# A two-layer kernel (a state-space layer, then an outlook-attention layer): where the first two attention tiles are made

## The chip, the core and the metric

The kernel runs on one core of a Trainium2 chip. The core has five engines that run their own instruction streams, each in the order in which it was given: PE (TensorE, the matrix multiplier; the profile shows its weight loads apart, as PEld), DVE (VectorE), ACT (ScalarE), POOL (GpSimd) and SP (SyncE), which here issues nearly all DMA transfers. They meet through semaphores only. Data lie in SBUF (on the chip, 128 partitions) and in HBM; matmuls write to PSUM, an accumulation memory of eight banks for each partition.

The metric is the time of one execution in microseconds on the device. Lower is better.

## What is computed

Input `x` is (4, 384, 64, 64) in float32. Two residual layers follow each other, each on a group norm of its input: a state-space layer over the 4096 pixels of an image, in sequence, and outlook attention on 3x3 windows with stride 2:

```python
    x = x + _L0_conv_ref(_gn(x), L0_conv_ln_w, L0_conv_ln_b, L0_conv_in_proj_w, L0_conv_conv_w, L0_conv_conv_b, L0_conv_x_proj_w, L0_conv_dt_w, L0_conv_dt_b, L0_conv_A_log, L0_conv_D, L0_conv_out_proj_w)
    x = x + _L1_conv_ref(_gn(x), L1_conv_attn_w, L1_conv_attn_b, L1_conv_conv_w, L1_conv_proj_w, L1_conv_proj_b)
```

Layer 0 normalises, projects 384 channels to twice 768, convolves along the sequence, makes step sizes `dt` and the vectors B and C, runs for each of 768 channels a scan with 16 states over 4096 steps (`h = dA * h + dBx`, `y = sum(h * C)`), gates it and projects back to 384.

Layer 1, cut to its core (12 heads of 32 channels, windows of 3x3 = 9 places, 32x32 windows in an image; `a` are the weights, `v` the values made from the patches with one matrix for each place, and the last addition is the fold, in which overlapping windows add up):

```python
        pooled = x.reshape(B, C, h, S, w, S).mean(axis=(3, 5))
        a = jnp.einsum('bchw,ac->bhwa', pooled, attn_w) + attn_b
        a = a.reshape(B, L, HEADS, K * K, K * K).transpose(0, 2, 1, 3, 4) * scale
        a = jax.nn.softmax(a, axis=-1)
...
        v = jnp.einsum('blkc,koc->blko', v, Wg)
        v = v.reshape(B, L, K * K, HEADS, hd).transpose(0, 3, 1, 2, 4)
        o = jnp.einsum('bnlpq,bnlqd->bnlpd', a, v)
...
                out = out.at[:, :, ki:ki + S * (h - 1) + 1:S, kj:kj + S * (w - 1) + 1:S].add(o[:, :, ki, kj])
...
        y = jnp.einsum('bchw,oc->bhwo', out, proj_w) + proj_b
```

The group norm at the head of layer 1 needs mean and variance of all that layer 0 gives for an image; so the last image's coefficients exist only when layer 0 is over, while those of the first three are there long before.

## The kernel before

**Layer 0** (`mamba_layer`) cuts each image's sequence into 17 chunks of 241 steps, 68 chunks in all. A chunk has 12 units of scan work (a unit: 2 groups of 32 channels with 16 states). The main loop (from L776) takes one step `s` for each unit. In a step DVE runs two scans (`s_scan`), ACT makes the decays of the next unit in two PSUM tiles `da0` and `da1` (`s_decay`, tiles from L559), POOL makes inputs and outputs (`s_inputs`, `s_outputs`), and every second step PE sums the states into `y` (`s_sum`) and DVE gates it (`s_gate`). SP fetches the inputs of two units four steps ahead (`s_fetch`: `dxr`, `dtr`). The front of a chunk (norm, projections, convolution) is laid into the steps of the chunks before by a table `plan`; what ends a chunk (`ends`: `e_project` with the output projection `ps_out` into `xr`, then `e_store` with the statistics and the store to `x1` in HBM) follows in the steps after it. `group_norm_coeffs` (L50) makes an image's coefficients `sc` and `bi` from these statistics: aggregation on DVE (`mv`), `pm` and `pv` on PE, a power on POOL, `bi` on ACT.

Engines work strictly in the order of the program text (class `InOrder`): an instruction that waits holds up all behind it on its engine, and a DMA that waits on SP all DMAs behind it.

**Layer 1** (`outlook_layer`) works on 32 tiles of 8 image rows (4 rows of windows, 128 windows). For a tile: load of 9 rows of `x1` as `xr` (864 KB; 768 KB for the first tile of an image), normed pixels `xp` (6 activations on ACT), pooled sums `t2` (3 additions on DVE), weights (`psa`: 6 matmuls, 12 in the records; softmax on DVE and ACT in tile `at`; store to an HBM tile `ad`), values (`psv`: 9 places of 3 matmuls, 54 records in all; copies on ACT; stores to `vd`). Then for each of the four rows of windows `r`: fetch of weights and values from HBM as `ain` and `vin`, a block-diagonal form `bd` of the weights (on ACT for even `r`, on POOL for odd `r`), products `ps` on PE, `fold` on DVE; last the projection `pso` and the output. The loop at L1085 takes three tiles at a time: it attends tile `i`, makes weights and values of tile `i+1`, and at `r == 2` the pixels of tile `i+2`. In an iteration PE has, in order: `psa` and the first three values of the next tile, `pso` of the tile before, products of `r = 0`, two values, products of `r = 1`, two values, and so on.

**Between them** stands the generator `outlook_before` (L1116). The main loop sends it on once in each step from `front_end` (step 803) to the last (step 839), through `behind` (L1206). By then the SBUF room of the fronts has been given back; the generator uses this room. It gets two PSUM buffers from the loop's pool `pmm`, which the projections use as well. Before, it loads tile 0 and the value matrices `wv`, makes pixels, values and pooled sums of tile 0, then those of tile 1, and then loads `wa` (1458 KB), `ab`, `wpr`, `pb`, `own` into the room that it used so far. In steps 814 and 815 the last units are scanned; the steps behind hold the last sums, gates, projections and the norm.

`outlook_layer` then starts with a scale of `wa` by 0.25 on DVE (L924) and, for tiles 0 and 1 (list `ready`), a second load of their rows for the residual and the weights (L1082), one tile after the other. The first iteration of the loop after that (`i = -1`) only fetches tile 0's weights and makes its first `bd`; the second (`i = 0`) attends tile 0, with no values to be made.

Of the kernel before, what the change touches and what calls it, by code (L numbers as in the profile page):

```python
# [7 lines left out]
F32 = mybir.dt.float32  # L8
# [4 lines left out]
P = 128  # L13
# [66 lines left out]
def mamba_layer(ctx, tc, x, w, x1, sc1, bi1, consts, behind):  # L80
# [475 lines left out]

    das = [pda.tile([P, NG * (1 + TM)], F32, tag=f"da{i}", name=f"da{i}") for i in range(2)]  # L559
    for da in das:  # L560
        ve.memset(da.rearrange("p (g s) -> p g s", g=NG)[:, :, 0:1], 0.0)
    bp = pbb.tile([P, 2, TM], F32, tag="bp", name="bp")
    ND = NG // 2
    units = {}
# [211 lines left out]
    for s in range(-4, NU * (len(chunks) + 2)):  # L776
        k, m = divmod(s, NU)
        if m % 2 == 0 and unit(s + 4) is not None:
            s_fetch(s + 4)
        parts(s, EARLY)  # L780
        if m % 4 == 3 or s >= NU * len(chunks):
            norm_part(False)

        if (u := unit(s + 1)) is not None:
            s_inputs2(u)
        if (u := unit(s - 3)) is not None and not u.first:
            s_gate(u)
        parts(s, READY)

        b, ci = chunks[k][:2] if 0 <= k < len(chunks) else (B, 0)  # L790
        if b + 1 < B:
            n, e = divmod(NU * ci + m - 3, NU // 2)
            if e == 0 and 0 < n <= NCB * NX:
                x_stat(b + 1, n - 1, pending.pop())
            if e == 1 and 0 <= n < NCB * NX:
                pending.append(x_load(b + 1, n))
            if e == 2 and n == NCB * NX:
                x_coeffs(b + 1)
        for i in range(2):
# [12 lines left out]
        norm_part(True)  # L812
        parts(s, POOL)
        if (u := unit(s + 2)) is not None:
            s_inputs(u)
        if (u := unit(s - 2)) is not None and not u.first:
            s_sum(unit(s - 3), u)
        parts(s, MID)
        parts(s, LATE)
        if s == front_end:  # L820
            fronts.close()
        if s >= front_end:
            behind(lambda: pmm.tile([P, 2, TM], F32, tag="mm", name="psv").rearrange("p a b -> p (a b)"))


NR = 4
# [3 lines left out]
class OutlookTile:  # L830
# [52 lines left out]
    def pool(self, ve, t2, t3):  # L883
# [13 lines left out]
def outlook_layer(ctx, tc, x1, w, out, sc1, bi1, weights, ready):  # L897
# [10 lines left out]
    NW = W // 2  # L908
    NT = H // (2 * NR)
    HO = HEADS * KK  # L910
    NA = HO * KK
    NH = NA // 2
    NGW = 3
    VQ = 3
    scale = float(HD) ** -0.5
    pe, ve, ae, gp, sp = (
        InOrder(tc, e) for e in (nc.tensor, nc.vector, nc.scalar, nc.gpsimd, nc.sync)
    )
# [1 line left out]
    wa, ab, wv, wpr, pb, own, vds, ads = (  # L920
        weights[name] for name in ("wa", "ab", "wv", "wpr", "pb", "own", "vds", "ads")
    )

    ve.tensor_scalar_mul(wa, wa, 0.25)  # L924
    io = ctx.enter_context(tc.tile_pool(name="io1", bufs=3))
    act = ctx.enter_context(tc.tile_pool(name="act1", bufs=2))
    pa = ctx.enter_context(tc.tile_pool(name="pa", bufs=1, space=bass.MemoryType.PSUM))
# [14 lines left out]
        c.pool(ve, t2, t3)  # L942

    def p_weights(c):

        psa = pa.tile([P, 2, 512], F32, tag="psa", name="psa")
        for h in range(2):
            for cb in range(NCB):
                pe.matmul(
                    psa[:, h, :NH],  # L950
                    c.t2[:, cb, :],
                    wa[:, cb, h * NH : (h + 1) * NH],
                    start=(cb == 0),
                    stop=(cb == NCB - 1),
                )
        at = act.tile([P, NA], F32, tag="at", name="at")
        ve.tensor_add(at.rearrange("p (h a) -> p h a", h=2), psa[:, :, :NH], ab.rearrange("p (h a) -> p h a", h=2))
        qs = at.rearrange("p (q a) -> p q a", q=KK)
        mx = act.tile([P, HO], F32, tag="mx", name="mx")
        ve.reduce_max(mx, at.rearrange("p (q a) -> p a q", q=KK), AX.X)  # L960
        ve.tensor_sub(qs, qs, mx.unsqueeze(1).to_broadcast([P, KK, HO]))
        ae.activation(at, at, AF.Exp, scale=scale)
        rs = act.tile([P, HO], F32, tag="rs", name="rs1")
        ve.reduce_sum(rs, at.rearrange("p (q a) -> p a q", q=KK), AX.X)
        ve.reciprocal(rs, rs)
        ve.tensor_mul(qs, qs, rs.unsqueeze(1).to_broadcast([P, KK, HO]))
        sp.dma_start(ads[c.i % 2][: P * KK, :].rearrange("(p q) a -> p (q a)", q=KK), at)

    def p_values(c, q):

# [108 lines left out]

        return (old, r) if r < NR else (mid, r - NR)  # L1080

    for c in ready:  # L1082
        p_load(c)
        p_weights(c)
    for i in range(-1, len(tiles) + 1):  # L1085
        new, mid, old = tile_at(i + 2), tile_at(i + 1), tile_at(i)
        for r in range(NR):
            if old and r == 0:
                p_fetch_values(old, 0)
            if old and r + 1 < NR:  # L1090
                p_fetch_values(old, r + 1)
            if mid and r == 0 and mid not in ready:
                p_weights(mid)
            c, k = ahead(old, mid, r + 2)
            if c:
                p_fetch_weights(c, k)
            c, k = ahead(old, mid, r + 1)
            qs = ((0, 1, 2), (3, 4), (5, 6), (7, 8))[r]
            for n, q in enumerate(qs):
                if c:  # L1100
                    p_blocks(c, k, n, len(qs))
                if mid and mid not in ready:
# [12 lines left out]

def outlook_before(ctx, tc, w, x1, H, W, sc1, bi1, dram, weights, ready):  # L1116


    nc = tc.nc
# [7 lines left out]
    t2s = [wp.tile([P, NCB, NR * NW], F32, tag=f"t2{i}", name=f"t2{i}") for i in range(2)]  # L1127
    with tc.tile_pool(name="before", bufs=1, side="right") as early:

        zero = early.tile([KK, C], F32, tag="zero", name="zero")  # L1130
# [4 lines left out]
        def load(i):  # L1135
            ready.append(OutlookTile(i, H, W))
            ready[i].load(sp, x1, early.tile([P, NCB, ROWS, W], F32, tag="xr", name="xr"))

        def pixels(i):
            return ready[i].pixels(gp, ae, early.tile([P, 3, NCB, ROWS, NW], F32, tag="xp", name="xp"), sc1, bi1)  # L1140

        def value(i, q):
            ps = psum()
            ready[i].values(pe, wv, q, ps[:, :C])
            v = early.tile([P, C], F32, tag="v", name="v", bufs=4)
            ae.copy(v, ps[:, :C])
            sp.dma_start(vds[i][: P * KK, :].rearrange("(p q) c -> p q c", q=KK)[:, q, :], v)

        load(0)
        made = pixels(0)  # L1150
        for q in range(KK):
            sp.dma_start(wv[:, :, q, :], w["wv"][:, :, q, :])
            if q % 2:
                psum = yield
                next(made, None)
        for i in range(2):
            if i == 1:
                for _ in pixels(1):
                    psum = yield
            for q in range(KK):  # L1160
                value(i, q)
                if q == 0 and i == 0:
# [6 lines left out]
            psum = yield  # L1169
    wp = ctx.enter_context(tc.tile_pool(name="wp1", bufs=1, side="right"))  # L1170
    na = HO * KK
    shapes = {
# [5 lines left out]
    }  # L1178
    for name, shape in shapes.items():
        weights[name] = wp.tile(shape, F32, tag=name, name=name)  # L1180
        sp.dma_start(weights[name], w[name])


@with_exitstack
def layers(ctx, tc, w, out):
# [17 lines left out]
    weights, ready = {}, []  # L1203
    later = outlook_before(ctx, tc, w, x1, H, W, sc1, bi1, dram, weights, ready)

    def behind(psum):  # L1206
        try:
            later.send(psum if started else None)
        except StopIteration:
            pass  # L1210
        started.append(True)
# [70 lines left out]
```

## Time and profile before

| | us |
|---|---|
| three runs | 6302.01, 6313.15, 6318.55 |
| their median | 6313.15 |
| the profiled execution, its own time | 6318.34 |
| its span in the profile | 6316.6 |

| engine | busy us in the whole span | share |
|---|---|---|
| PE | 5629.0 | 89% |
| DVE | 5369.9 | 85% |
| POOL | 5311.1 | 84% |
| ACT | 4986.2 | 79% |

| event of the stage between the layers | us from the start |
|---|---|
| first transfer for layer 1 (tile 0's rows) issued | 4968.96 |
| first value of tile 0 on PE | 4993.27 |
| last value of tile 1 ends on PE | 5064.30 |
| load of `wa` issued | 5067.64 |
| coefficients of the last image (`bi`) done | 5080.49 |
| second load of tile 0's rows issued | 5080.52 |
| first attention product `ps` of tile 0 | 5115.99 |
| first attention product of tile 1 | 5153.89 |
| first attention product of tile 2 | 5191.75 |
| end of the span | 6316.6 |

How to read the lines further down: `L45` is the line of the helper through which all engines' instructions go, so tiles tell the operations apart, by the names above. `out<-in` is followed by the shapes and `xN`, the number of instructions in the group. A float32 matmul leaves two records. In brackets stands how long the engine had been idle before, and what released it. PEclk is the clock that the core granted to PE, as a share of full speed.

### The profile page before, as it was taken

The numbers are of one execution on the slowest core, as the hardware profiler recorded it, in microseconds if no ns is written. First come the engines' busy times: TensorE is split into PE (matmuls) and PEld (weight loads), VectorE is DVE, ScalarE is ACT, GpSimd is POOL, SyncE is SP. The second block draws the span as 40 slices with busy tenths as digits, with TensorE's granted clock in tenths as the row PEclk, the third lists the DMA queues.
The fourth block names the chain that finished last, engine by engine and source line by source line (L and its number), as shares of the span: only waits on it lengthen the run. The fifth ranks groups of instructions, "written<-read, shape, count | busy, mean of one in ns | idle before, by whom it ended". The sixth has DMA issues, their size and how long they took to land.

```text
span 6316.6 us, 113361 instructions
## 1 busy us (share of the span) xinstructions
PE 5629.0 (89%) x40488; PEld 3968.2 (63%) x40488; DVE 5369.9 (85%) x4784; ACT 4986.2 (79%) x11842; POOL 5311.1 (84%) x2047
## 2 busy tenths in 40 slices
PE   6888888898888888888888898988988779999999
PEld 5666666666666666666666666666666445555555
DVE  4999999999999999999999999999999844544444
ACT  3888888888898888888888888989888734444453
POOL 3999999999999999999999999999999924333333
PEclk9899989999998999999999989999999789999999
DMA  4555555455555555555555455554555544445544
GB/s 129 130 133 146 149 130 137 128 138 141 146 131 143 135 136 137 135 131 145 136 146 148 122 135 131 140 139 125 137 129 137 154 144 164 166 166 171 169 165 143
DMA packets 640987, 895.10 MB, mean 142 GB/s; under 512 B 130265, under 2 KB 535179, under 8 KB 640164
## 3 DMA queue, kind: packets, MB, share of 16 engines
q1 hardware_dynamic: 640420, 887.84, 51.5%
q8 instruction: 319, 5.23, 0.4%
q14 instruction: 248, 2.03, 0.1%
HBM read 661.78 MB, written 225.70 MB: 141 GB/s over the span
## 4 chain that ended last, share of the span: by engine, by line
PE 23%; ACT 17%; DVE 11%; issue 3%; DMA 1%; POOL 1%; SPq 1%; ACTq 0%; DVEq 0%; POOLq 0%
ACT da L45 10%; DVE h L45 8%; PE psv L45 6%; PE pso L45 4%; PE ps L45 4%; PE psa L45 3%; PE y L45 2%; PE ps_in L45 1%; ACT xc L45 1%; DVE at L45 1%; PE ps_xd L45 1%; DVE mx L45 1%; ACT L45 1%; POOL h L45 1%; ACT dt L45 1%
## 5 line engine op out<-in xcount | busy, mean ns | idle before, releaser
L45 DVE TENSOR_TENSOR_SCAN h<-da,h 128x968 f32<-128x968 f32 x1632 | 3449.4, 2154 | 80.9 <-issue 52.7
L45 ACT ACTIVATE da<-dtr,aneg 128x241 f32<-128x241 f32 x6528 | 3036.5, 465 | 291.9 <-DVE h L45 128.4
L45 POOL TENSOR_TENSOR h<-h,bc 128x1928 f32<-128x1928 f32 x816 | 3228.2, 3956 | 11.0 <-DVE h L45 8.8
L45 POOL TENSOR_TENSOR h<-dxr,bc 128x964 f32<-128x964 f32 x816 | 1625.6, 1992 | 116.8 <-PE y L45 101.3
L45 PE MATMUL ps_in<-u,win 128*128 128x241 f32 x4896 | 1079.6, 374 | 82.0 <-DVE dtx L45 75.1
L45 PEld LDWEIGHTS ps_in<-u,win 128*128 128x128 f32 x4896 | 911.6, 191 | 247.8 <-DVE dtx L45 98.8
L45 POOL TENSOR_TENSOR bd<-ain,own 99x1188 f32<-99x1188 f32 x192 | 412.1, 2175 | 748.7 <-DMA ain<-ad 553.5
L45 DVE TENSOR_TENSOR h<-dxr,bp 128x964 f32<-128x964 f32 x816 | 928.4, 1138 | 113.5 <-PE y L45 97.9
L45 PE MATMUL y<-h,ssum 128*32 128x241 f32 x13056 | 909.2, 406 | 24.3 <-POOL h L45 23.1
L45 PEld LDWEIGHTS y<-h,ssum 128*32 128x32 f32 x13056 | 433.5, 119 | 441.8 <-issue 213.0
L45 PE MATMUL ps_cv<-xb,cdiag 128*128 128x241 f32 x3264 | 694.2, 368 | 5.8 <-ACT neg L45 4.7
L45 PEld LDWEIGHTS ps_cv<-xb,cdiag 128*128 128x128 f32 x3264 | 610.9, 189 | 78.9 <-issue 13.5
L45 PE MATMUL ps_xd<-xc,wx 128*56 128x241 f32 x816 | 306.6, 556 | 323.3 <-ACT xc L45 323.3
L45 PE MATMUL psv<-wv,xp 128*128 128x384 f32 x1728 | 588.9, 492 | 0.0
L45 ACT ACTIVATE bd<-ain,own 99x324 f32<-99x324 f32 x704 | 334.4, 555 | 298.6 <-PE ps L45 289.4
L45 PE MATMUL ps_out<-zs,wout 128*128 128x241 f32 (+1 forms) x2448 | 536.8, 368 | 0.0
L45 DVE TENSOR_TENSOR fold<-fold,ps 128x192 f32<-128x192 f32 (+1 forms) x768 | 211.1, 303 | 352.8 <-PE ps L45 327.3
L45 PEld LDWEIGHTS ps_out<-zs,wout 128*128 128x128 f32 x2448 | 470.2, 192 | 36.9
L45 PEld LDWEIGHTS psv<-wv,xp 128*128 128x128 f32 x1728 | 320.9, 190 | 224.2 <-issue 8.4
L45 PEld LDWEIGHTS ps_xd<-xc,wx 128*56 128x56 f32 x816 | 154.0, 198 | 464.2 <-ACT xc L45 348.8
L45 PE MATMUL ps_dt<-xd,wdt 25*128 25x241 f32 x816 | 255.9, 440 | 113.0 <-ACT dt L45 79.4
L45 PE MATMUL y<-xc,ddiag 128*128 128x241 f32 x816 | 279.4, 427 | 10.2 <-DVE zs L45 10.2
(106 smaller groups left out, 5370.2 us busy)
## 6 DMA issues: line engine op xcount, KB each, us to landing
dxr<-dxd SPq DMA_DIRECT2D x1632, 120.5 KB
dtr<-dtd SPq DMA_DIRECT2D x1632, 120.5 KB
bc<-bcd SPq DMA_DIRECT2D x544, 120.5 KB
vin<-vd SPq DMA_DIRECT2D x384, 148.5 KB
vd<-vst SPq DMA_DIRECT2D x90, 576.0 KB
dxd<-dtx SPq DMA_DIRECT2D x272, 180.8 KB
dtd<-dt SPq DMA_DIRECT2D x272, 180.8 KB
xr<-x SPq DMA_DIRECT2D x87, 288.0 KB
```

Of the source, the lines that this page charges most:

```text
L45: return self.tc.keep_in_program_order(issue(*args, **kwargs))
```

## The change

Five edits, all around the joint of the layers:

- Tile 0 alone is made ahead: values, pooled sums, and now its weights with the softmax too. Tile 1 goes through the loop of `outlook_layer` as all others do.
- The weights' matmuls of tile 0 go into `da0` (padded from 968 to 1024 elements, so that its halves are two banks), handed over from step 815 on, when the last scan has read it. They are issued in step 815, between the sums of units 813 and 815; the softmax and the store to `ad` are issued in step 819, behind the statistics of chunk 66 and ahead of the last chunk's projections. The buffers `at`, `mx`, `rs` come from the generator's own pool.
- `wa` and the other weights of layer 1 are loaded as soon as tile 0 is through (step 812, was 820), `wa` in three parts. The four zero fills of `vd` and `ad` are issued at the head, ahead of the loads of `wv`.
- The scale of `wa` is dropped; the factor 0.25 goes into the addition of the bias (`scalar_tensor_tensor` in place of `tensor_add`).
- In `outlook_layer` nothing stands ahead of the loop any more. In its first iteration (`i = -1`) it loads tile 1 at `r = 0` and makes its pixels there (other tiles: `r = 2`), and loads tile 0's rows for the residual at `r = 1`. In the second (`i = 0`) it makes weights and values of tile 1, beside the attention of tile 0.

```diff
-    das = [pda.tile([P, NG * (1 + TM)], F32, tag=f"da{i}", name=f"da{i}") for i in range(2)]
+    das = [pda.tile([P, 1024], F32, tag=f"da{i}", name=f"da{i}") for i in range(2)]
...
-            behind(lambda: pmm.tile([P, 2, TM], F32, tag="mm", name="psv").rearrange("p a b -> p (a b)"))
+            over = das[0] if s >= NU * len(chunks) - 1 else None
+            behind(lambda: pmm.tile([P, 2, TM], F32, tag="mm", name="psv").rearrange("p a b -> p (a b)"), over)
...
+    def weights(self, pe, ve, ae, sp, psa, pool, wa, ab, ad):
+        HO = HEADS * KK
+        NH = HO * KK // 2
+        for h in range(2):
+            for cb in range(NCB):
+                pe.matmul(
+                    psa[:, h, :NH],
+                    self.t2[:, cb, :],
+                    wa[:, cb, h * NH : (h + 1) * NH],
+                    start=(cb == 0),
+                    stop=(cb == NCB - 1),
+                )
+        yield
+        at = pool.tile([P, 2 * NH], F32, tag="at", name="at")
+        ve.scalar_tensor_tensor(
+            at.rearrange("p (h a) -> p h a", h=2),
+            psa[:, :, :NH],
+            0.25,
+            ab.rearrange("p (h a) -> p h a", h=2),
+            ALU.mult,
+            ALU.add,
+        )
+        qs = at.rearrange("p (q a) -> p q a", q=KK)
+        mx = pool.tile([P, HO], F32, tag="mx", name="mx")
+        ve.reduce_max(mx, at.rearrange("p (q a) -> p a q", q=KK), AX.X)
+        ve.tensor_sub(qs, qs, mx.unsqueeze(1).to_broadcast([P, KK, HO]))
+        ae.activation(at, at, AF.Exp, scale=float(HD) ** -0.5)
+        rs = pool.tile([P, HO], F32, tag="rs", name="rs1")
+        ve.reduce_sum(rs, at.rearrange("p (q a) -> p a q", q=KK), AX.X)
+        ve.reciprocal(rs, rs)
+        ve.tensor_mul(qs, qs, rs.unsqueeze(1).to_broadcast([P, KK, HO]))
+        sp.dma_start(ad[: P * KK, :].rearrange("(p q) a -> p (q a)", q=KK), at)
...
-    ve.tensor_scalar_mul(wa, wa, 0.25)
...
-    for c in ready:
-        p_load(c)
-        p_weights(c)
...
+            if i < 0 and r == 1:
+                for c in ready:
+                    p_load(c)
-            if r == 2 and new and new not in ready:
+            if r == (0 if i < 0 else 2) and new and new not in ready:
                 p_pixels(new)
```

In `outlook_before` (the loop over tiles 0 and 1 is replaced by tile 0 alone):

```diff
+        for i in range(2):
+            sp.dma_start(vds[i][P * KK :, :], zero)
+            sp.dma_start(ads[i][P * KK :, :], zero[:, :HO])
+        made = c.pixels(gp, ae, early.tile([P, 3, NCB, ROWS, NW], F32, tag="xp", name="xp"), sc1, bi1)
...
-        for i in range(2):
-            if i == 1:
-                for _ in pixels(1):
-                    psum = yield
-            for q in range(KK):
-                value(i, q)
-                if q == 0 and i == 0:
-                    load(1)
-                if q % 2:
-                    psum = yield
-            ready[i].pool(ve, t2s[i], early.tile([P, NCB, NR * NW], F32, tag="t3", name="t3"))
-            sp.dma_start(vds[i][P * KK :, :], zero)
-            sp.dma_start(ads[i][P * KK :, :], zero[:, :HO])
-            psum = yield
+        for q in range(KK):
+            ps = psum()
+            c.values(pe, wv, q, ps[:, :C])
+            v = early.tile([P, C], F32, tag="v", name="v", bufs=4)
+            ae.copy(v, ps[:, :C])
+            sp.dma_start(vds[0][: P * KK, :].rearrange("(p q) c -> p q c", q=KK)[:, q, :], v)
+            if q % 2:
+                psum, over = yield
+        c.pool(ve, t2, early.tile([P, NCB, NR * NW], F32, tag="t3", name="t3"))
+        yield
...
+    for cb in range(NCB):
+        sp.dma_start(weights["wa"][:, cb], w["wa"][:, cb])
+    for name in ("ab", "wpr", "pb", "own"):
         sp.dma_start(weights[name], w[name])
+    while True:
+        psum, over = yield
+        if over is not None:
+            break
+    parts = c.weights(
+        pe, ve, ae, sp, over.rearrange("p (h a) -> p h a", h=2), wp, weights["wa"], weights["ab"], ads[0]
+    )
+    next(parts)
+    for _ in range(4):
+        yield
+    next(parts, None)
```

More of the change, by code (lines that the diff above doesn't have):

```diff
@@ L554, in parts @@
                     part(chunk(k))
-    das = [pda.tile([P, NG * (1 + TM)], F32, tag=f"da{i}", name=f"da{i}") for i in range(2)]
+    das = [pda.tile([P, 1024], F32, tag=f"da{i}", name=f"da{i}") for i in range(2)]
     for da in das:
-        ve.memset(da.rearrange("p (g s) -> p g s", g=NG)[:, :, 0:1], 0.0)
+        ve.memset(da[:, : NG * (1 + TM)].rearrange("p (g s) -> p g s", g=NG)[:, :, 0:1], 0.0)
     bp = pbb.tile([P, 2, TM], F32, tag="bp", name="bp")
@@ L910, in outlook_layer @@
     HO = HEADS * KK
-    NA = HO * KK
-    NH = NA // 2
     NGW = 3
     VQ = 3
-    scale = float(HD) ** -0.5
     pe, ve, ae, gp, sp = (
@@ L946, in p_weights @@
         psa = pa.tile([P, 2, 512], F32, tag="psa", name="psa")
[L947 to L967, printed above, removed]
+        for _ in c.weights(pe, ve, ae, sp, psa, act, wa, ab, ads[c.i % 2]):
+            pass
     def p_values(c, q):
@@ L1126, in outlook_before @@
     wv = weights["wv"] = wp.tile([P, NCB, KK, C], F32, tag="wv", name="wv")
-    t2s = [wp.tile([P, NCB, NR * NW], F32, tag=f"t2{i}", name=f"t2{i}") for i in range(2)]
+    t2 = wp.tile([P, NCB, NR * NW], F32, tag="t2", name="t2")
+    c = OutlookTile(0, H, W)
+    ready.append(c)
     with tc.tile_pool(name="before", bufs=1, side="right") as early:
+        c.load(sp, x1, early.tile([P, NCB, ROWS, W], F32, tag="xr", name="xr"))
         zero = early.tile([KK, C], F32, tag="zero", name="zero")
@@ L1133, in outlook_before @@
         ads = weights["ads"] = [dram.tile([P * KK + KK, HO], F32, tag=f"ad{i}", name=f"ad{i}") for i in range(2)]
[L1135 to L1150, printed above, removed]
+        for i in range(2):
+            sp.dma_start(vds[i][P * KK :, :], zero)
+            sp.dma_start(ads[i][P * KK :, :], zero[:, :HO])
+        made = c.pixels(gp, ae, early.tile([P, 3, NCB, ROWS, NW], F32, tag="xp", name="xp"), sc1, bi1)
         for q in range(KK):
@@ L1153, in outlook_before @@
             if q % 2:
-                psum = yield
+                psum, over = yield
                 next(made, None)
-        for i in range(2):
-            if i == 1:
-                for _ in pixels(1):
-                    psum = yield
-            for q in range(KK):
-                value(i, q)
-                if q == 0 and i == 0:
-                    load(1)
-                if q % 2:
-                    psum = yield
-            ready[i].pool(ve, t2s[i], early.tile([P, NCB, NR * NW], F32, tag="t3", name="t3"))
-            sp.dma_start(vds[i][P * KK :, :], zero)
-            sp.dma_start(ads[i][P * KK :, :], zero[:, :HO])
-            psum = yield
+        for q in range(KK):
[8 more added lines that the diff above has]
+        yield
     wp = ctx.enter_context(tc.tile_pool(name="wp1", bufs=1, side="right"))
@@ L1180, in outlook_before @@
         weights[name] = wp.tile(shape, F32, tag=name, name=name)
+    for cb in range(NCB):
+        sp.dma_start(weights["wa"][:, cb], w["wa"][:, cb])
+    for name in ("ab", "wpr", "pb", "own"):
         sp.dma_start(weights[name], w[name])
+    while True:
+        psum, over = yield
+        if over is not None:
[7 more added lines that the diff above has]
+    next(parts, None)
 @with_exitstack
@@ L1204, in layers, with behind @@
     later = outlook_before(ctx, tc, w, x1, H, W, sc1, bi1, dram, weights, ready)
-    def behind(psum):
+    def behind(*room):
         try:
-            later.send(psum if started else None)
+            later.send(room if started else None)
         except StopIteration:
```

## The prediction

> **What bounds the kernel now.** I read the table by stage first, then the chain of waits and the timeline in the stage between the two layers, because the change touches nothing else. In the table the columns are: stretch, its length, busy time and (number of instructions) of PE, PEld, DVE, ACT and POOL, granted clock, DMA share, GB/s.
>
> ```profile
> core 0: us, PE busy (x) PEld busy (x) DVE busy (x) ACT busy (x) POOL busy (x), PEclk, DMA share, GB/s
> 5022.00:5043.70 21.70, 12.20 (x87) 5.04 (x78) 20.57 (x13) 18.77 (x45) 21.06 (x8) 0.71 0.04 15
> 5043.70:5064.30 20.60, 20.60 (x91) 12.06 (x90) 3.25 (x8) 3.94 (x9) 4.32 (x2) 0.97 0.22 76
> 5064.30:5080.50 16.20, 12.38 (x62) 11.25 (x61) 4.53 (x8) 2.33 (x7) 1.85 (x1) 0.85 0.63 220
> 5080.50:5116.00 35.50, 12.82 (x26) 5.18 (x25) 16.29 (x12) 7.14 (x13) 4.58 (x3) 0.69 0.36 113
> 5116.00:5153.90 37.90, 31.40 (x338) 20.64 (x338) 17.59 (x35) 16.43 (x32) 17.98 (x11) 0.72 0.33 102
> 5153.90:5191.75 37.85, 37.78 (x373) 21.64 (x372) 18.83 (x36) 18.80 (x38) 14.62 (x9) 1.00 0.51 174
> 5191.75:6275.50 1083.75, 1081.09 (x10795) 626.70 (x10795) 530.19 (x1039) 538.20 (x1092) 416.95 (x256) 1.00 0.49 166
> ```
>
> The last scan steps are POOL's (21.06 of 21.70). The next 20.6 are PE's alone. From 5064.3 to 5116 no engine is near full: that is a chain of waits. From 5153.9 on PE is full (37.78 of 37.85 in a period of one tile). So there are 52 us in which work may be moved at no cost, and behind them a PE that pays for all that it is given; but the tile before it (5116 to 5153.9) took a whole period for less work (PE 31.40).
>
> The chain of waits (start, length, work) names the pieces; those left out are given below in words:
>
> ```profile
> 5043.72 8.54 PE psv L45 x24
> 5052.26 2.17 PE y L45 x34
> 5054.43 9.87 PE psv L45 x30
> 5064.31 8.57 PE ps_out L45 x42
> ...
> 5080.23 7.93 PE psa L45 x12
> ...
> 5115.99 3.15 PE ps L45 x72
> ```
>
> The psv of these 18.41 us are the values of the second tile, all of them; they stand ahead of the last projections (ps_out), and so of the last norm. Then one after the other: statistics, coefficients (bi ends at 5080.49), weights and softmax of tile 0, softmax of tile 1, fetch of ain, first attention product ps at 5115.99.
>
> The timeline gives when things come free (start, length, engine):
>
> ```profile
> 4973.41 0.41 POOL L45 MEMSET zero<- 9x384 f32 x1
> 5018.75 6.76 SPq L45 DMA_DIRECT2D vd<-v  x3
> 5036.29 11.74 POOL L45 TENSOR_TENSOR h<-h,bc 128x1928 f32<-128x1928 f32 x3
> 5080.52 1.27 SPq L45 DMA_DIRECT2D xr<-x  x3
> 5124.25 4.13 ACT L45 ACTIVATE xp<-xr,bi,sc 128x465 f32<-128x465 f32 x6
> 5172.79 5.16 PE L45 MATMUL psa<-wa,t 128*128 128x486 f32 x12
> ```
>
> **The change part by part**, on this execution's clock (span 6316.6, time 6318.34 with 1.74 around it; 5.2 above the median of 6313.15).
>
> (1) The tail of PE. The second tile's psv go, 8.54 and 9.87. In place of the first group stands psa of tile 0 (12 records, into da0). It needs wa: its load now follows the last vd store on SP (issued by 5025.5), and 2.5 MB at the 360 to 390 GB/s of 5068 to 5076 is 7 us, so it is there by 5036 and PE comes at 5043.7. Warm, psa is 5.16; the 24 psv after the same wait took 8.61 where 12 warm ones take 4.14, so 0.3 is added: 5.5, to 5049.2. POOL ends at 5048.03, so y runs 5049.2 to 5051.4, and ps_out follows at once: 5051.4 for 5064.31, a gain of 12.9. If psa takes its cold 7.93, 2.4 less.
>
> (2) Softmax of tile 0 ahead of the residual copies. On DVE, in order: zs 0.4, statistics 1.0, at 1.2 (scalar_tensor_tensor in place of tensor_add; for 512 elements it takes 0.745, so about 1.2 for 972), mx 1.95, subtraction 1.17, to 5057.1; exp on ACT 1.01, to 5058.1. Behind exp wait the three copies of ps_out: the first ends at 5058.5, not 5054.6. ps_out has two buffers, so its third part waits: 5058.5 + 2.85 + 0.37 = 5061.7. DVE meanwhile needs 1.94 + 0.83 + 1.17 after exp, to 5062.1, then two statistics and the third: 5063.3. Before, the third ended at 5073.71: the gain is now 10.4, so the softmax gives 2.5 back. The store of ad is issued on SP ahead of the last x1 store: at most its own 1.5 us on a store that landed in 4.5; it stays under the 6.8 of the next step.
>
> (3) Aggregation, pm, pv, root and bi are not changed: 5073.71 to 5080.49 is 6.78, so bi ends at 5070.1.
>
> (4) The prologue. Between bi and the first ps were 35.5 us, softmax twice. Now, in series: load of tile 1 (864 KB; SP waits for bi as before; the 768 KB issued at 5080.52 were moved by 5084.1, that is 3.6; with 0.3 for the size and 0.5 for the semaphore 4.4), pixels on ACT 4.15, three additions 2.0, psa cold 7.93, nine values 18 records 6.0, waits 0.3: 24.8, ps at 5094.9. The bd of tile 0 (5.12 on ACT behind the pixels) ends near 5084, its ain is there by then: covered by psa, and if that cover were gone it would cost its 5.12. psa is the uncertain term: the same 12 records took 6.26 at 5134.81.
>
> The Trainium skill, "TensorE: Matmul & The Clock Gate", Part 1, says that after an idle window of about 3.4 us the array runs at half clock until it has been busy for about such a window. By it psa, all of it after 12 idle us, would lose about 1.7 and take 6.9, and the sum would be 1 better; the row at 5080.23 lost 2.8, and I keep the row. [...]
>
> (5) The first period. The second tile's values (18.4) and weights (5.2) now lie where PE is paid for, but this stretch was 37.9 already, held up by DVE's fold and ACT's bd. A full period is 37.85, and the first pso is 7.04 for 8.00: 36.9. Without a pso ahead of the first ps, tile 1's softmax ends 3.4 after it, not 3.3 before. SP holds behind its ad store the ain of r=2 (landing about 7.3 after ps), so bd of r=2 ends near 13.1 where ps would want it at 11.5, and the pixels of tile 2 follow late: I take 2.0. Bounds: 0, and 6.44 (a whole bd group of POOL). Second tile's first ps: 5094.9 + 38.9 = 5133.8 for 5153.89.
>
> (6) Moved for nothing, as far as I see: four zero fills go ahead of the wv loads. SP waits for POOL's memset (ends 4973.82, where wv was issued at 4970.37) and issues four at 0.35: everything behind, wv and two dxr/dtr fetches, is up to 4.9 late. The nearest fetch (issued 4971.74) is wanted by POOL at 4984.0, the next (4981.95) at 4995.65, and its landing was near 4990: slack about 5, so I take 0; bounds 0 and 4.9. POOL, the bound there, would lose it. The 864 KB that leave this stage give nothing back. The scale of wa (1.68) goes, folded into (2). The scans' da tiles only get padding. From 5153.9 on nothing changes.
>
> Sum: 5153.9 - 5133.8 = 20.1 earlier; 6318.34 - 20.1 = 6298.2, and on the median 6313.15 - 20.1 = **6293.0**, 0.32% less. The bounds: all small terms good (psa 6.26, no stall in (5), load 0.4 less) gives 4.1 more, 6289; all bad (2.4 + 4.4 + 4.9 and 1.5 of store) takes 13.2, 6306. The runs shown lie 11 below to 5 above their median, so low reaches to 6283.
>
> **Rivals.**
> - The second tile's start stalls. Its load, pixels and sums now stand in series with the first product, and its queue on SP is late in (5). For: each link waits on the one before, and 5064 to 5116 was such a chain. Against: all needed rows are short. Price: stall 6.4 for 2.0 and 3 in the chain: 6300.5.
> - The zero fills reach the scan. For: DMA engines full from 4970 to 4995 (share 1.00). Against: the slack above. Price 4.9: 6298.
> - Slower: the last y held by wa. psa stands ahead of it on PE in order, and wa ahead of ab and wpr behind the vd stores on SP. For: wa's load was issued at 5067.64 before, and DVE could use it only at 5078.45. If it came as late now, y would wait 5043.7 to 5078.5, 34.8 for 5.5: 29.3 lost, 6322. It turns the sign once wa lands 20 after 5049, so once it is issued after about 5058. Against: SP is free at 5025.5, and tile 0's sums on DVE ended at 5021.6.
> - It doesn't do as it says: tile 0's softmax still ends behind the norm, since ab or the space comes late; the tail gains, the prologue keeps one softmax of 9.3: 6302.
>
> **How the numbers follow.** Forecast 0.66; stalled start 0.17; zero fills 0.09; slower 0.04; not as it says 0.04. A difference of 0.3%, 18.9 us, is about what this kernel's measurement tells from no change; it lies at 6294.2, close to my forecast. With some 5 us for the terms and the runs, two thirds of the forecast's chance is below it: 0.44; the three middle cases add 0.06. So faster 0.50, slower 0.05 (nearly all of that rival and a little for what I haven't seen), the same 0.45. Range 6283 to 6306: above it lie the slower rival and the ends of the stalled ones, below it a gain over 30 for which no term is left.
>
> **What would show it.** (1) psa between the last two y on PE, with no wait for wa, and ps_out 12 to 13 earlier against the last scan. (2) exp ahead of the three xr copies; third statistics about 10 earlier. (4) about 25 between bi and the first ps. (5) 38 to 41 between first ps of tile 0 and of tile 1, PE nearly full. (6) the scans to 5043 where they were. It is wrong if ps of tile 0 comes later than 33 us after bi, if the scan steps after 4970 stretch, or if the period after 5153.9 moves from 37.85.

## The result, and the profile after

| | before | after |
|---|---|---|
| median us | 6313.81 (20 runs) | 6299.24 (20 runs) |
| lowest to highest | 6302.01 to 6327.04 | 6283.41 to 6306.58 |
| ratio of the times, 95% interval | | 0.9972 [0.9965, 0.9979] |
| profiled execution, time / span | 6318.34 / 6316.6 | 6291.97 / 6289.9 |

The change makes the kernel about 15 us faster, 0.28%: inside the range, 6.2 above the forecast. The forecast's 20.1 of 6313.15 is a ratio of 0.9968, which lies in the interval too. The forecast took 0.3%, 18.9 us, as about the least that can be told from no change, and gave 0.45 to a gain below it; the gain lies there, but with 20 runs of each kernel the interval still tells it from no change. The times alone can't say whether 20.1 was right; the traces can.

The two profiled executions must first be brought to one time base. In the kernel before, the first of the last four scans starts at 5034.61, after at 5022.60. All of these 12 us are there earlier, where the instructions are still the same: the scan of unit 804 starts at 4971.47 and 4958.79. That is scatter of the main loop (the changed kernel, profiled again further down, has its last scans at 5034.63). So everything below counts from an event in the same trace. The joint, from the start of the last four scans to tile 1's first `ps`, took 119.28 us (5034.61 to 5153.89) and takes 105.03 (5022.60 to 5127.63): **the joint gives 14.25, not 20.1**.

The table by stage of the changed kernel, cut at the same events as the one of before (columns as there):

```profile
core 0: us, PE busy (x) PEld busy (x) DVE busy (x) ACT busy (x) POOL busy (x), PEclk, DMA share, GB/s
5010.00:5031.50 21.50, 12.05 (x86) 4.79 (x75) 20.57 (x13) 15.19 (x40) 20.87 (x7) 0.72 0.45 152
5031.50:5039.60 8.10, 8.10 (x48) 3.86 (x46) 0.41 (x1) 0.00 (x0) 4.42 (x2) 0.89 0.00 0
5039.60:5056.50 16.90, 12.30 (x64) 10.77 (x60) 12.03 (x17) 2.64 (x7) 0.64 (x2) 0.92 0.14 52
5056.50:5086.30 29.80, 13.03 (x34) 6.50 (x35) 11.37 (x7) 10.42 (x21) 8.58 (x4) 0.65 0.30 95
5086.30:5127.60 41.30, 37.56 (x373) 21.54 (x372) 24.57 (x38) 19.40 (x41) 14.92 (x9) 1.00 0.46 152
5127.60:5165.50 37.90, 37.84 (x373) 21.70 (x372) 18.50 (x36) 18.88 (x38) 14.61 (x9) 1.00 0.51 176
5165.50:6249.20 1083.70, 1081.18 (x10796) 626.75 (x10796) 528.37 (x1040) 538.48 (x1092) 417.13 (x256) 1.00 0.49 166
```

Second row: PE's tail is 8.1 us where it was 20.6. Fourth: the prologue is 29.8 for 35.5. Fifth: tile 0's attention now takes 41.3, longer than the full period of 37.9 behind it, though PE does no more work (37.56 and 37.84). The last row is the one of before.

The timeline of the changed kernel at the tail and in the prologue (start, length, engine, operation, count, idle time before it and its releaser):

```profile
5031.55 5.96 PE L45 MATMUL da<-wa,t 128*128 128x486 f32 x12
5037.35 0.57 PE L45 MATMUL y<-xc,ddiag 128*128 128x241 f32 x2
5037.85 1.84 PE L45 MATMUL y<-h,ssum 128*32 128x241 f32 x32
5039.62 0.67 PE L45 MATMUL ps_out<-xr,ident 128*128 128x241 f32 x2
...
5045.38 1.01 ACT L45 ACTIVATE at<-at 128x972 f32<-128x972 f32 x1 [14.00 <-DVE at L45]
...
5046.30 0.61 ACT L45 COPY xr<-ps_out 128x241 f32<-128x241 f32 x2
...
5055.62 0.55 POOL L45 TENSOR_TENSOR sc<-sc,mhalf 128x1 f32<-128x1 f32 x1 [19.71 <-DVE sc L45]
...
5062.20 4.06 ACT L45 ACTIVATE xp<-xr,bi,sc 128x465 f32<-128x465 f32 x6 [5.69 <-DMA xr<-x]
...
5065.69 7.06 POOL L45 TENSOR_TENSOR bd<-ain,own 99x1188 f32<-99x1188 f32 x3 [9.42 <-DMA ain<-ad]
5066.17 5.10 ACT L45 ACTIVATE bd<-ain,own 99x324 f32<-99x324 f32 x11
5066.35 4.38 DVE L45 TENSOR_TENSOR t<-xp 128x384 f32<-128x384 f32 x2 [10.80 <-DMA vin<-vd]
5070.76 2.41 DVE L45 TENSOR_TENSOR t<-t,t 128x384 f32<-128x384 f32 x1
```

`psa` of tile 0 (`da<-wa,t`) stands where the forecast put it, with no wait for `wa`. The exponential stands ahead of the copies of `ps_out`, as forecast. In the last two rows the three small additions of tile 1's pixels take 6.8 us on DVE, while POOL makes `bd` beside them. In the trace of before the same three took 1.6 (5055.77 to 5057.37), with POOL idle:

```profile
5055.77 1.01 DVE L45 TENSOR_TENSOR t<-xp 128x384 f32<-128x384 f32 x2
5056.81 0.56 DVE L45 TENSOR_TENSOR t<-t,t 128x384 f32<-128x384 f32 x1
```

The order of PE in tile 0's attention, after:

```profile
5086.27 1.77 PE L45 MATMUL ps<-bd,vin 99*32 99x99 f32 x72
...
5096.73 2.20 PE L45 MATMUL psv<-wv,xp 128*128 128x384 f32 x6 [0.82 <-ACT vst L45]
5100.28 1.90 PE L45 MATMUL ps<-bd,vin 99*32 99x99 f32 x72 [1.35 <-ACT vst L45]
...
5108.63 0.69 PE L45 MATMUL ps<-bd,vin 90*32 90x90 f32 x24 [1.18 <-POOL bd L45]
5109.63 5.16 PE L45 MATMUL psa<-wa,t 128*128 128x486 f32 x12 [0.32 <-DVE t L45]
```

PE waits four times, for copies, blocks and sums that should have been ready. The same stretch on SP's queue says why they were late:

```profile
5063.77 2.81 SPq L45 DMA_DIRECT2D vin<-vd  x6
5090.19 0.35 SPq L45 DMA_DIRECT2D ad<-at  x1
5090.58 1.51 SPq L45 DMA_DIRECT2D ain<-ad  x3
...
5094.53 1.20 SPq L45 DMA_DIRECT2D vin<-vd  x3
5095.83 1.37 SPq L45 DMA_DIRECT2D ain<-ad  x3
```

For 24 us, until 5090.19, SP issues nothing: it stands at the store of tile 1's softmax, and the fetches for tile 0's third and fourth row groups stand behind it.

### The profile page after: what moved, and what is told of

The parts are those of the page before. It is cut to its first block, busy times and chain, and to the rows that moved or that the text cites. A ratio compares the mean times of both kernels' runs of the same rounds, so it can differ in the third digit from the quotient of the medians.

```text
span 6289.9 us, 113342 instructions
## 1 busy us (share of the span) xinstructions
PE 5605.3 (89%) x40488; PEld 3949.3 (63%) x40488; DVE 5373.2 (85%) x4783; ACT 4985.3 (79%) x11842; POOL 5310.6 (84%) x2047
## 5 line engine op out<-in xcount | busy, mean ns | idle before, releaser
L45 PEld LDWEIGHTS ps_cv<-xb,cdiag 128*128 128x128 f32 x3264 | 611.0, 189 | 79.9 <-issue 13.5
```

The source lines that it names most:

```text
L45: return self.tc.keep_in_program_order(issue(*args, **kwargs))
```

## The experiments

All readings of the table are from traces, each from events of its own trace. "Additions" are the three on DVE for tile 1's pooled sums, from first start to last end; "to first `ps`" runs from the end of `bi` to tile 0's first `ps`; "period" from there to tile 1's.

| kernel | additions | to first `ps` | period | both |
|---|---|---|---|---|
| before | (tile 1 ahead) | 35.50 | 37.90 | 73.40 |
| after | 6.82 | 29.77 | 41.36 | 71.13 |
| after, again (e9) | 6.37 | 29.48 | 41.07 | 70.55 |
| e1 blocks on ACT | 1.62 | 23.12 | 43.36 | 66.48 |
| e2 fetches ahead | 6.44 | 29.23 | 36.92 | 66.15 |
| e3 softmax in layer 1 | 1.63 | 30.74 | 41.22 | 71.96 |
| e4 zero fills back | 6.83 | 29.81 | 43.77 | 73.58 |
| e5 load ahead | 1.62 | 19.20 | 41.87 | 61.07 |
| e6 = e1' + e2 | 1.63 | 25.49 | 36.94 | 62.43 |
| e7 = e1' + e2 + e5 | 1.62 | 18.42 | 36.93 | 55.35 |
| e8 a scale of `wa` | 6.76 | 29.18 | 41.25 | 70.43 |
| e10 = e2 + e5 | 1.62 | 19.09 | 36.89 | 55.98 |
| e11 = e7 again | 1.62 | 19.24 | 36.91 | 56.15 |

**e1: POOL away from the additions.**

```diff
+        if c.i == 0 and r == 1:
+            if part == 0:
+                for k in range(GW):
+                    ae.mul(bd[:, :, k, :], c.ain[r], own[:, k : k + 1])
-        if r % 2 == 0:
+        elif r % 2 == 0:
```

> The blocks of row group 1 of tile 0 are made on ACT instead of POOL, so that POOL makes no blocks beside tile 1's three additions. Theory (POOL's blocks slow DVE's additions): the additions fall from 6.8 us to 1.6 to 2.5 us, psa of tile 1 starts 4 to 5 us sooner after bi, and the first ps of tile 0 comes 24.5 to 26 us after the end of bi instead of 29.8. Rival (the additions are slow because xp is freshly written, or because of the transfers of ain and vin that run then): they stay at 6 to 7 us and the first ps stays 29 to 30 us after bi.

Timeline of e1 at the additions:

```profile
5068.86 5.10 ACT L45 ACTIVATE bd<-ain,own 99x324 f32<-99x324 f32 x11
5069.04 1.03 DVE L45 TENSOR_TENSOR t<-xp 128x384 f32<-128x384 f32 x2 [9.94 <-ACT xp L45]
5070.10 0.56 DVE L45 TENSOR_TENSOR t<-t,t 128x384 f32<-128x384 f32 x1
```

The additions take 1.62, beside the same 5.10 us of ACT that reads the same `ain`. `xp` is as freshly written as before, and the transfers run as before (198 GB/s from 5069 to 5071), so neither is the reason. The theory holds. The first `ps` comes even 6.65 sooner; 5.2 of it are the additions, the rest a load (4.83 for 5.69) and a `psa` (6.68 for 7.26) that happened to be shorter. But the period grew by 2.0: the eleven blocks had been placed behind the exponential of tile 1's softmax on ACT (5082.79 to 5087.90), and the copies of tile 1's values waited behind them (PE idle 3.37 on `vst`). The cure was put in the wrong place; e6 moves it.

**e2: the fetches ahead of the store.**

```diff
-            if old and r + 1 < NR:
+            if old and r + 1 < NR and not (i == 0 and r == 1):
...
+            if i == 0 and r == 0:
+                p_fetch_weights(old, 2)
+                p_fetch_values(old, 2)
+                p_fetch_weights(old, 3)
...
-            if c:
+            if c and not (i == 0 and r < 2):
                 p_fetch_weights(c, k)
```

> The fetches of ain for row groups 2 and 3 of tile 0 and of vin for row group 2 are issued ahead of the store of tile 1's softmax. Theory (the stall in the first period is SP waiting for tile 1's softmax): from the first ps of tile 0 to the first ps of tile 1 it takes 37 to 38.5 us instead of 41.4, and the idle time of PE that ends on ACT's vst before the second ps (0.8 and 1.35 us) and on POOL's bd (1.18 us) goes. Rival (the copies and blocks on ACT are the limit, not the fetch): the period stays within 0.7 us of 41.4. The time from bi to the first ps stays 29 to 30 us in both.

PE in tile 0's attention, e2:

```profile
5103.65 1.75 PE L45 MATMUL ps<-bd,vin 99*32 99x99 f32 x72
5105.33 4.14 PE L45 MATMUL psv<-wv,xp 128*128 128x384 f32 x12
5109.39 1.76 PE L45 MATMUL ps<-bd,vin 99*32 99x99 f32 x72
5111.09 4.14 PE L45 MATMUL psv<-wv,xp 128*128 128x384 f32 x12
5115.15 1.76 PE L45 MATMUL ps<-bd,vin 99*32 99x99 f32 x72
```

Not one wait is left, and the period is 36.92. ACT and POOL do the same work as after; only SP's order differs. The theory holds, the rival falls.

**e3: is the early softmax worth anything?** Tile 0's `psa` and softmax go back into layer 1; tile 1's values stay out of the tail.

```diff
-    parts = c.weights(
...
-    next(parts)
-    for _ in range(4):
-        yield
-    next(parts, None)
...
             if i < 0 and r == 0:
+                for c in ready:
+                    p_weights(c)
```

> The psa and the softmax of tile 0 are made in the second layer again, behind the load of tile 1, and the values of tile 1 stay out of the tail. Theory (the softmax in the tail takes 2.5 us of the chain of statistics, and it would be hidden beside tile 1's load and pixels): the third statistics come 2 to 3 us sooner behind the last scan than in the changed kernel (28.8 us), and the first ps of tile 0 comes no later behind bi than 30 us, 25 to 27 us if the additions are then no longer beside POOL's blocks. Rival (the softmax in the tail is what shortens the prologue): the first ps of tile 0 comes 33 us or more behind bi, since the softmax holds DVE and SP ahead of the additions and the fetches.

The aggregation of the third statistics starts 26.36 behind the first of the last four scans (5026.30 to 5052.66) instead of 28.70: the 2.5 of step (2), measured as 2.34, is real. But the prologue is 0.97 longer, though the additions are fast again: on ACT the exponential of tile 0 stands ahead of the pixels, which start 11.3 behind `bi`:

```profile
5058.27 0.29 ACT L45 ACTIVATE bi<-neg,sc 128x1 f32<-128x1 f32 x1 [2.88 <-POOL sc L45]
5068.90 1.01 ACT L45 ACTIVATE at<-at 128x972 f32<-128x972 f32 x1 [10.34 <-DVE at L45]
5069.82 4.09 ACT L45 ACTIVATE xp<-xr,bi,sc 128x465 f32<-128x465 f32 x6
```

30.74 lies between the two expectations (at most 30; 33 or more), so the run decides less than hoped. From the last scans to tile 1's `ps` e3 takes 104.22, after 105.03: as placed, the early softmax brings nothing. What is left as the gain is what e3 keeps: tile 1's values and weights made beside tile 0's attention, and no longer in the tail and in a row behind tile 0's. That holds only while POOL is beside the additions. In e1 they are as fast as in e3, and there the early softmax pays: from the last scans to tile 0's first `ps` e1 takes 57.01, e3 63.00 (of the 6.0 between them, 1.2 are e3's `psa` of tile 1, 7.90 against 6.68).

**e4: zero fills back** behind the values of tile 0 (one loop of three lines moved).

> The zero fills of the two scratch tensors go back behind the values of tile 0. Theory (ahead of wv they hold SP for 0.4 to 0.7 us of the scan steps): from the scan of unit 804 to the last scan it takes 63.1 us, as in the kernel before, instead of 63.8. Rival (noise of the last steps): it stays 63.5 to 64.

63.62 from the scan of unit 804 to the last scans (4964.49 to 5028.11): the rival's figure. With the fills ahead, after, e1, e2 and e3 show 63.81, 63.54, 63.54 and 63.67. The fills cost nothing that can be seen. Why the one execution of before shows 63.14 stays open. The period of 43.77 in this run, in code that the edit does not touch, ends on a transfer of `vin` that came late (PE idle 2.75): with SP in its old order tile 0's attention varies by over 2 us (41.07 to 43.77 in the table).

**e5: the load of tile 1 in the tail**, into room of its own; `wpr` moves to the second layer's pool and is loaded later, tile 0's dead `t2` serves as `t3`.

```diff
+    weights["xr1"] = wp.tile([P, NCB, ROWS, W], F32, tag="xr1", name="xr1")
...
+    OutlookTile(1, H, W).load(sp, x1, weights["xr1"])
...
-                if new and new not in ready:
+                if i < 0:
+                    new.xr = weights["xr1"]
+                elif new and new not in ready:
                     p_load(new)
```

> Tile 1's pixels are loaded in the tail, into room of their own (wpr and t3 give up theirs and are placed elsewhere). Theory (the 5.7 us from bi to the pixels are the load, and nothing else holds them): the pixels start within 0.5 us of the end of bi, the additions are over before POOL's blocks begin and take 1.6 to 2.5 us, and the first ps of tile 0 comes 19.5 to 21 us behind bi instead of 29.8. Rival (the blocks of tile 0, whose fetches still start behind bi, come last once the load is gone): the first ps comes 23 us or more behind bi, with PE idle on ACT's or POOL's bd or on vin ahead of it.

Timeline of e5 (`bi` ends at 5059.58):

```profile
5063.62 1.03 DVE L45 TENSOR_TENSOR t<-xp 128x384 f32<-128x384 f32 x2 [4.99 <-ACT xp L45]
5064.68 0.56 DVE L45 TENSOR_TENSOR t<-t,t 128x384 f32<-128x384 f32 x1
...
5065.59 5.12 ACT L45 ACTIVATE bd<-ain,own 99x324 f32<-99x324 f32 x11 [2.06 <-DMA vin<-vd]
5065.89 6.43 POOL L45 TENSOR_TENSOR bd<-ain,own 99x1188 f32<-99x1188 f32 x3 [6.54 <-DMA ain<-ad]
```

The pixels now start at 5059.49, as soon as `bi` is written. POOL's `bd` is there as in the changed kernel, but starts 0.65 after the additions end: they are fast without being touched, and `bd` takes 6.43 instead of 7.06. The first `ps` comes 10.6 sooner.

**e6: both cures**, the blocks on ACT now directly behind those of row group 0 (called e1' in the table).

```diff
+            if i < 0 and r == 3:
+                p_blocks(mid, 1, 0, 1)
```

> Both cures at once: the blocks of row group 1 of tile 0 on ACT, this time put right behind those of row group 0, ahead of the exponential of tile 1's softmax, and the fetches of row groups 2 and 3 ahead of the store of that softmax. Theory (the two losses are independent, 6.6 us before the first ps and 4.4 us behind it): first ps of tile 0 at 23 to 24 us behind bi, first ps of tile 1 another 36.9 to 37.5 us later, together 60 to 61.5 us against 71.1. Rival (they share a cause, so that the second cure adds nothing to the first): together 65 us or more.

The period is 36.94, so the moved blocks cost nothing any more. The first `ps` is at 25.49, 1.5 over the expectation: the load took 6.11 and `psa` with the values 13.5 (e1: 4.83 and 12.42). Together 62.43 lies between the theory's 61.5 and the rival's 65; against e1's 23.12 and e2's 36.92, together 60.0, the 2.4 more are these two scattering terms, so the losses are separate ones.

**e7: all three.**

> The three at once: blocks on ACT, fetches ahead, tile 1's pixels loaded in the tail. Theory: first ps of tile 0 at 19.5 to 21 us behind bi, first ps of tile 1 at 56.5 to 58.5 us behind bi against 71.1; the kernel takes 13 to 14.5 us off the changed kernel, so a ratio to the kernel before of 0.9945 to 0.9955. Rival (the blocks on ACT or the fetches now end last): 60 us or more behind bi, ratio 0.9957 or above.

From `bi` to tile 1's `ps` ("both") it takes 55.35, one better than expected, 15.78 below the changed kernel's. The ratio of 0.9966 [0.9952, 0.9979] lies above the 0.995 that this should give, and where the rival put it (0.9957 or above), though 55.35 is far from the rival's 60. The next three runs, all on one chip, take this up.

**e8: the scale of `wa`, with 1.0.** One term had come out better than forecast: `bi` 5.1 behind the third statistics instead of 6.8. The trace of before shows POOL's power beside the scale of `wa` on DVE:

```profile
5078.32 1.85 POOL L45 TENSOR_TENSOR sc<-sc,mhalf 128x1 f32<-128x1 f32 x1 [30.29 <-DVE sc L45]
5078.45 1.68 DVE L45 TENSOR_SCALAR wa<-wa 128x2916 f32<-128x2916 f32 x1 [0.22 <-DMA x<-xr]
```

```diff
+    ve.tensor_scalar_mul(wa, wa, 1.0)
     io = ctx.enter_context(tc.tile_pool(name="io1", bufs=3))
```

> A multiplication of wa by 1.0 is put on DVE where the kernel before had its multiplication by 0.25 (one operation of 128 x 2916, 1.68 us there), with nothing waiting for its result but tile 1's psa. Theory (that operation on DVE held up POOL's power sc beside it, 1.85 us before and 0.55 us after): sc takes 1.7 to 1.9 us again and bi ends 1.2 to 1.4 us later behind the third statistics (6.3 to 6.6 us instead of 5.1). Rival (POOL was slow for a reason of its own, such as its first use of the operation): sc stays at 0.5 to 0.6 us and bi does not move.

e8:

```profile
5073.60 1.68 DVE L45 TENSOR_SCALAR wa<-wa 128x2916 f32<-128x2916 f32 x1
5073.73 1.96 POOL L45 TENSOR_TENSOR sc<-sc,mhalf 128x1 f32<-128x1 f32 x1 [19.74 <-DVE sc L45]
```

POOL's operation of one element for each partition takes 1.96, and ends 0.4 behind the operation of DVE beside it; in every run without that operation it takes 0.55. `bi` ends 6.57 behind the start of the aggregation instead of 5.20 (5.16 to 5.90 in the other runs). The theory holds.

**e9, e10, e11: the changed kernel, e2 + e5, and e7 again, on one chip.** e10 has the diffs of e2 and e5 alone.

> The changed kernel as it is, beside the next two on one chip. Theory (the joint gives 13.6 to 14.3 us and the main loop is the same but for its own scatter): ratio to the kernel before 0.9977, with an interval that holds it. Rival (something of the change also moves the main loop): the interval lies below 0.9972 or above 0.9985.

> Fetches ahead and tile 1's pixels loaded in the tail, with the blocks of row group 1 left on POOL. Theory (without the load ahead of them the additions are over before POOL's blocks begin, so these need not go to ACT): first ps of tile 0 at 18.5 to 20 us behind bi, first ps of tile 1 at 55.5 to 57 us behind bi; the time lies 14 to 16 us below the changed kernel's. Rival (POOL's blocks meet tile 2's additions or hold the second ps): 58 us or more behind bi.

> The version with all three cures once more, beside the changed kernel on the same chip: its profile showed the joint 15.8 us shorter than the changed kernel's, but its ratio of 0.9966 is only 0.0006 below the changed kernel's. Theory (that was the scatter of the main loop from run to run): median 11 to 18 us below the changed kernel's. Rival (the gain is given back somewhere outside the joint): within 7 us of the changed kernel's, and a stretch of the trace outside the joint that is longer by what is missing.

| | median us | ratio to before |
|---|---|---|
| before, same chip | 6314.05 | |
| e9 (the changed kernel) | 6302.47 | 0.9979 [0.9969, 0.9988] |
| e10 | 6285.10 | 0.9949 [0.9938, 0.9961] |
| e11 | 6291.88 | 0.9956 [0.9943, 0.9969] |

e9's interval holds the 0.9978 that a joint shorter by some 14 us gives. e10 lies 17.4 below e9 and e11 10.6, around the 14.6 and 14.4 by which their "both" is shorter than e9's. Each lies just outside what was expected of it (14 to 16, and 11 to 18): the two medians differ by 6.8 where "both" differs by 0.2, so six runs don't tell a median to a few us. The traces can say more. From tile 1's first `ps` to the end of the span, before, after, e7, e9, e10 and e11 take 1161.5 to 1162.9, so nothing is given back there; and the last scans start at 5019.14 in e7 and at 5043.52 in e11, which are the same kernel. So the gain is not given back, and e7's ratio lies within the scatter of the main loop. With the load ahead, POOL's blocks may stay on POOL: three fetches and a load moved forward (e10) beat both kernels.

## Why the prediction was right, and where not

The mechanism was right; two terms of the sum were mis-sized, and one came out better, which was luck: the forecast had nothing for it. The range held the miss, but through terms that did not happen (`psa` cold in the tail, the zero fills, the store: 8.8 of its 13.2); the additions were not among them. By the prediction's steps (forecast, measured):

- **(1)** `psa` in the tail 5.5; 5.96, with no wait for `wa` (issued at 5015.26; the 360 to 390 GB/s taken for its load are those of 5070 to 5076, from 5068 to 5070 there were 181). `ps_out` at 5051.4; 5039.62, which is 5051.63 on the time base of before (12.01 added). Right.
- **(2)** Third statistics end 5063.3; 5051.38, that is 5063.39. Right, by the order that was forecast, and e3 measures the softmax's price as 2.34 for 2.5.
- **(3)** 6.78 from there to the end of `bi`, taken as unchanged; 5.12. The scale of `wa` was booked as 1.68 of DVE that "goes"; what it also did was to hold POOL's power in the chain. The power took 1.85 and takes 0.55, so this is 1.3 of the 1.7, and e8 brings it back; the rest are the first `pv` matmuls on PE, 1.29 before and 0.93 after.
- **(4)** 24.8 from `bi` to the first `ps`; 29.77. **This step failed, at "three additions 2.0"**: 6.8. The row behind the 2.0 had POOL idle beside it. That POOL would make `bd` of row group 1 just then followed from the same step, which has tile 0's `ain` there early; I looked at the `bd` on ACT only. e1, e3 and e5 each take POOL's `bd` away from the additions, by engine or by time, and each time they take 1.6. The other terms: load 5.7 for 4.4; `psa` 7.26 for 7.93, with the nine values 13.0 for 14.2. The 4.4 had 0.5 for the semaphore in it, and the lower bound a load shorter by 0.4; no run shows either term, and the seven loads behind `bi` kept ACT waiting for 4.83 to 6.11. Not only that the sum is 5.0 off, but by which row, is thus shown.
- **(5)** 36.9 without a stall: e2, e6, e7, e10 and e11 show 36.89 to 36.94. The stall was taken as 2.0 and is 4.4, and the period of 41.36 lies just over the 38 to 41 that the prediction gave as its sign. The cause was named ("SP holds behind its ad store the ain of r=2"), the size was wrong: row group 3's `ain` and the `vin` of row group 2 stand in the same queue, POOL's `bd` for row group 3 came later still (5101.82), and tile 2's additions met that `bd` (4.32 for two, at 5104.67).
- **(6)** 0; at most 0.7, and e4 shows none of it to be the zero fills.

Sum: 20.1 + 1.6 from (3) - 5.0 from (4) - 2.4 from (5) is 14.3; the trace has 14.25.

Of the rivals, "the second tile's start stalls" priced its two losses at 7.4 over the forecast, and (4) and (5) lost 7.4. Its time of 6300.5 is 1.3 off, but the 6298 of the zero fills, which cost nothing, is 1.2 off: only the traces tell the two apart. The stalled start had the place right, and the queue, but not the additions. The zero fills, the wait for `wa` and "it doesn't do as it says" did not happen.

## What to carry to other kernels

A duration is a duration in company: before an instruction is moved, look at what the other engines will do at its new place, and above all at POOL when it is one of DVE's with two inputs in SBUF. When a value is made later than before, look at the queue in which its store stands: what is fetched behind it is late as well, and the cure is an order, not a faster engine. And where a change is worth less than the scatter of the runs, measure from event to event in one trace, and bring different executions to one time base first.

## What the hardware showed that I had not expected

**DVE and POOL take turns.** The two engines' instructions in the changed kernel, one by one:

```profile
5065.69 2.17 POOL L45 TENSOR_TENSOR bd<-ain,own 99x1188 f32<-99x1188 f32 x1 [9.42 <-DMA ain<-ad]
5066.35 1.93 DVE L45 TENSOR_TENSOR t<-xp 128x384 f32<-128x384 f32 x1 [10.80 <-DMA vin<-vd]
5067.82 2.49 POOL L45 TENSOR_TENSOR bd<-ain,own 99x1188 f32<-99x1188 f32 x1
5068.20 2.52 DVE L45 TENSOR_TENSOR t<-xp 128x384 f32<-128x384 f32 x1
5070.27 2.48 POOL L45 TENSOR_TENSOR bd<-ain,own 99x1188 f32<-99x1188 f32 x1
5070.76 2.41 DVE L45 TENSOR_TENSOR t<-t,t 128x384 f32<-128x384 f32 x1
```

Each addition ends 0.4 behind one of POOL's multiplications and takes 1.93 to 2.52 instead of 0.55; POOL's second and third are longer too (2.49 and 2.48 for 2.17). So each of DVE's operations pays for one of POOL's, not for all three. ACT's eleven operations on the same `ain` in the same time do not disturb DVE (1.62 in e1, 1.60 before). A profile shows such a wait as busy time: no bracket names it.

The Trainium skill states this rule, on the page "SBUF — State Buffer", section Who interferes with whom: a DVE instruction with two SBUF inputs contends with a GpSimd instruction that reads SBUF, and the one that comes second is held until the other ends. This trace agrees, with 0.55 turned into 1.93 to 2.52. The same section says that `tensor_scalar` can take the shared ports in a faster mode; the power of 1.85 and 1.96 beside it, 0.55 alone, agrees with that. In the trace of before POOL's record starts 0.13 ahead of DVE's (5078.32 and 5078.45), and POOL is the one held all the same: the records' starts don't show which engine had the ports first.

**A cold `psa` scatters.** Tile 1's `psa`, twelve records that take 5.16 warm, comes behind 6.9 to 19.4 us of idle time in the changed kernel and all its variants, and takes 6.57 (e8) to 7.90 (e3) in these twelve executions. The granted clock shows where the time goes: it is 0.50 from the start of `psa` on, for about 2.9 us in e8, 4.3 in the changed kernel and 5.6 in e3, and then 1.00; the loss of 1.4, 2.1 and 2.7 is about half of that. The forecast's 7.93 and the 6.9 that it put beside it lie at either side of the 7.26 of the changed kernel. The 6.9 came from the Trainium skill, "TensorE: Matmul & The Clock Gate", Part 1: half clock until a window of about 3.4 us has been busy, from which a loss of 1.7 is an estimate. The same Part says that the window runs free, so that the point of change varies. These rows show it to vary by more than the estimate tells: losses of 1.4 to 2.7.

**The main loop scatters by more than the change is worth.** The changed kernel's last scans start at 5022.60 in one profiled execution and at 5034.63 in another, at mean granted clocks of 0.936 and 0.934; in e11, with 0.930, at 5043.52.
